# A Mamba, deformable-convolution, Fourier and attention stack on one core: the last image kept in SBUF between layers, its sampling positions made in two halves, and table stores of two chunks at a time

## The chip, the cores and the metric

The kernel runs on one core of a Trainium2 chip. The metric is the device time in microseconds of one execution, the median of several runs, lower is better. The core has five instruction queues that run side by side: PE (TensorE, matmuls), DVE (VectorE), ACT (ScalarE), POOL (GpSimd) and SP (SyncE, which only issues DMAs). Each of them runs its instructions in the order in which the program put them, and waits on semaphores for the others.

## What is computed

Four images of 96 channels and 64 by 64 pixels pass through four layers. Cut to what matters here:

```python
def reference(x, ...):                      # x: (4, 96, 64, 64)
    # layer 0: norm, projection, 3x3 depthwise conv, a selective scan in 4 directions
    #   h[t] = exp(delta[t] * A) * h[t-1] + delta[t] * u[t] * B[t];  y[t] = sum(h[t] * C[t])
    #   then norm, gate silu(z), projection;            x1 = x + layer0(x)
    # layer 1: group norm, then a deformable 3x3 convolution:
    n = group_norm(x1)
    off, mask = conv(n, offset_w), sigmoid(conv(n, mask_w))   # 9 taps for every pixel
    s = bilinear(n, base + off) * mask      # four neighbours of each of 9 positions
    x2 = x1 + einsum(weight, s) + bias
    # layer 2: t = x2;  t += fourier_mlp(norm(t));  t += quantized_ffn(norm(t))
    # layer 3: t += linear_attention(norm(t));      t += quantized_ffn(norm(t))
    return t
```

## The kernel before, in words

A channel-major image `[96, 4096]` is handled in eight chunks of 512 pixels (`CH`). Three streams of work are laid into the five queues by a planner that runs while the program is built. The first is the scan of layer 0 (`scan`): 1536 units, each one exponential on ACT (L1014), one product on DVE (L1034), one scan on DVE (L1042), one product on POOL (L1051) and matmuls (L1020, L1070). The second (`ends`) prepares the inputs of the scan for the next images, and then runs layers 2 and 3 of image 0, 1, 2, 3 in turn. The third (`middle`) runs, for each image in turn, what follows its scan (`behind`, which ends layer 0) and layer 1 (`Layer1.image`). A step of a stream carries an estimated cost, and `Clock.has_room` decides by it when a step is put in. `pipe` interleaves several chains of one stream; a chain takes and frees named slots (`takes`, `frees`). Nothing is put in a new order when the program runs.

For one image, the third stream does the following.

- `behind` works in four groups of two chunks, from the last chunks to the first. It loads the column-scan result of direction 3 with the axes exchanged (`yta`, `ytc`, L1112: for each channel and each of 64 columns one short run of rows), once for each half of the image. It adds that on POOL to the row result (L1134), norms, multiplies by the gate on POOL (L1180), projects, adds `x` (L1189) and stores `x1` to DRAM (L1191).
- `offsets` loads `x1` back (L1246), takes the group norm's statistics (eight `bn_stats`, L448), norms on ACT in place (L1260) and copies on POOL into a padded image (L1262). Then, for each chunk: nine matmuls of the offset convolution (L1278), and a transpose of the pixels, copied to `pix` (L1297) and stored eight times into a DRAM table (L1310), in which every pixel's entry holds its four neighbours (two tables, used in turn by the images). `pix` has two buffers.
- `positions` turns the offsets of the whole image into table indices `idx` and weights `wt`: one sigmoid on ACT (L1330) and sixteen operations on DVE (L1334 to L1363).
- `sample` gathers with an indirect DMA on POOL (L1383), 288 of them for an image, each of 128 pixels for one tap; weights them; transposes on PE (L1416); copies to `st` (L1424); multiplies by the convolution's weights (L1432); adds `x1`, loaded again by 256 pixels (L1429), on DVE (L1437); and stores `x2` (L1439). `g`, the gathered pixels, has six buffers of three taps; `st` has one.

Layers 2 and 3 begin with a load of the whole `x2` (L1825). Then comes a norm over the channels (`normed`: centring matmuls L485, sums of squares L501, Ln and Exp on ACT, three operations on DVE, spreading matmuls L527, a product L1613), and the Fourier part (L1551, L1510, L1576, L1590, L1595).

Only the last image has nothing to hide behind: when its scan is over, its layer 1 runs beside the layers 2 and 3 of image 2, and its own layers 2 and 3 run alone.

Of the kernel before, what the change touches and what calls it, by code (L numbers as in the profile page):

```python
# [8 lines left out]
F32 = mybir.dt.float32  # L9
# [262 lines left out]
def pipe(net, chains, width, every=0, lane=None, **tiles):  # L272
# [5 lines left out]
    while True:  # L278
# [9 lines left out]
        for n, chain in enumerate(active):  # L288
# [8 lines left out]
            if not all(free[tag] > 0 for tag in chain.takes):  # L297
                continue
# [5 lines left out]
        for tag in chain.takes:  # L304
            free[tag] -= 1
# [54 lines left out]
class Net:  # L360
# [3 lines left out]
    def __init__(self, ctx, tc, ins):  # L364
# [20 lines left out]
        self.sampling_last = False  # L385
        self.clock, self.known, self.streams, self.stream = Clock(), {}, [], None
# [56 lines left out]
    def group_norm_stats(self, x, pool, key, stats):  # L443

        nc = self.nc
        st = pool.tile([C, NCH, 6], F32, name=f"gnst{key}", tag="gnst")
        for j in range(NCH):
            nc.vector.bn_stats(st[:, j, :], x[:, j * CH : (j + 1) * CH])  # L448
            if j % 2:
                yield cost(dve=1.4)  # L450
# [22 lines left out]
    def centred(self, x, cen, dst, key, pool, bias=None, groups=(0, 1)):  # L473
# [7 lines left out]
        def chain(j):  # L481
            yield wait(new=True, takes="sq")
# [72 lines left out]
class Layer0:  # L555
# [438 lines left out]

    def fetch_step(self, u):
# [96 lines left out]
    def behind(self, b):  # L1092
# [6 lines left out]
        with (  # L1099
# [3 lines left out]
            cen_a, cen_c, wo_a, wo_c = (net.load(q, big) for q in ("cen_a", "cen_c", "wo_a", "wo_c"))  # L1103
            for j0 in range(NCH - HB, -1, -HB):
                if j0 % (NCH // 2) == NCH // 2 - HB:

                    h0 = H // 2 * (j0 * 2 // NCH)
                    yta = big.tile([128, W, H // 2], F32, name=f"yta{b}_{h0}", tag="yta")
                    ytc = big.tile([D2, W, H // 2], F32, name=f"ytc{b}_{h0}", tag="ytc")
                    for yt, c0 in ((yta, 0), (ytc, 128)):  # L1110
                        src = self.y_d[b][3][c0 : c0 + yt.shape[0]].rearrange("c (w h) -> c w h", h=H)
                        nc.sync.dma_start(yt, src[:, :, h0 : h0 + H // 2])  # L1112
                    yta_v, ytc_v = (t.rearrange("p w h -> p h w") for t in (yta, ytc))
                    yield wait(4.0)
                while not all((b, 2, j * CH // T) in self.summed for j in range(j0, j0 + HB)):
                    yield BLOCKED
                ca = big.tile([128, HB, CH], F32, name=f"ca{b}_{j0}", tag="ca")
# [5 lines left out]
                def centred(i):  # L1123
# [8 lines left out]
                    for y, yt in ((ya, yta_v), (yc, ytc_v)):  # L1132
                        y = y.rearrange("p (h w) -> p h w", w=W)
                        nc.gpsimd.tensor_add(y, y, yt[:, rs, :])  # L1134
                    yield cost(pool=3.1, new=True)
# [22 lines left out]
                nw = op.tile([128, CH], F32, name=f"nw{b}_{j0}", tag="nw", bufs=1)  # L1158
# [3 lines left out]
                def gated(i):  # L1162
# [16 lines left out]
                    for o, n, z, vg, vb in parts:  # L1179
                        nc.gpsimd.tensor_mul(o[:, i, :], o[:, i, :], z)  # L1180
# [760 lines left out]
```

## Time and profile before

| quantity | value |
|---|---|
| median of the 3 runs shown | 8472.4 us (8467.96 to 8479.75) |
| the profiled execution's own time | 8455.38 us |
| its span, first to last instruction | 8453.6 us |
| busy share of the span: PE, DVE, ACT, POOL | 76%, 81%, 58%, 66% |
| last unit of the scan starts on DVE | 7416.3 us |
| last `x1` of image 3 stored | 7481.0 us |
| first to last gather of image 3 starts | 7590.3 to 8023.3 us |
| image 2 written out | 7905.2 us |
| image 3's Fourier part begins | 8076.1 us |

The durations come from one profiled execution, which took 17 us less than the median of the runs. Times in the text are microseconds from the start of its span. The share of busy time mixes stages with different limits: up to 7416 the scan rules, after it the work of the last images.

### The profile page before, as it was taken

The page shows a single profiled execution, that of the slowest core. Times are in us where ns is not written, and L with a number is a line of the kernel's source. Part 1 is how long each engine was busy: PE and PEld are TensorE (multiplying, and loading weights), DVE is VectorE, ACT ScalarE, POOL GpSimd, SP SyncE. Part 2 cuts the span into 40 slices and gives each one's busy share as a digit, 9 for nine tenths or more (in the row PEclk, how much of TensorE's full clock was granted, in tenths as well). Part 3 has the DMA queues.
Part 4 walks back from the last instruction along what each step waited for, and adds up shares of the span by engine and source line. Part 5 has one row for each costly group of instructions (what it writes and reads, how often), then busy time and mean ns, then how long its engine had stood idle before and what let it go on. Part 6 is the DMA issues. An engine that isn't in the chain of part 4 may idle for free.

```text
span 8453.6 us, 96209 instructions
## 1 busy us (share of the span) xinstructions
PE 6424.4 (76%) x31848; PEld 2772.6 (33%) x31848; DVE 6826.4 (81%) x5122; ACT 4914.8 (58%) x8979; POOL 5621.2 (66%) x4308
## 2 busy tenths in 40 slices
PE   6765787678766777977767889777788777797587
PEld 2211221112222223321222555222455232464273
DVE  2799889987789898779888898898898988838714
ACT  5665566555567777855566677645576876333224
POOL 1566566665568888856578898766798997627700
PEclk8776787678767778977667898786798787898698
DMA  3676678877679888877788999776899897744410
GB/s 98 169 209 186 166 190 214 204 186 188 171 205 241 233 235 220 230 187 198 194 216 233 236 237 245 184 177 175 224 239 235 216 228 188 187 111 138 142 60 17
DMA packets 773926, 1608.27 MB, mean 190 GB/s; under 512 B 264082, under 2 KB 355758, under 8 KB 771223
## 3 DMA queue, kind: packets, MB, share of 16 engines
q10 hardware_dynamic: 244224, 843.17, 39.2%
q1 hardware_dynamic: 455478, 532.37, 24.4%
q0 software_dynamic: 73728, 226.57, 10.1%
q8 instruction: 256, 4.19, 0.2%
q14 instruction: 240, 1.96, 0.1%
HBM read 1345.43 MB, written 256.29 MB: 189 GB/s over the span
## 4 chain that ended last, share of the span: by engine, by line
PE 32%; DVE 26%; DMA 12%; POOL 11%; issue 9%; ACT 8%; SPq 2%; ACTq 1%; DVEq 0%; POOLq 0%
DVE da L1042 12%; POOL da L1051 7%; DVE db L1034 7%; PE pc L763 3%; DMA da<-de 3%; PE py L1070 3%; PE ps L1416 3%; PE f L1510 3%; POOL g L1383 3%; PE pd L1432 2%; PE db L1020 2%; ACT g L1395 2%; ACT da L1014 2%; DMA du<-du 1%; PE h L1551 1%
## 5 line engine op out<-in xcount | busy, mean ns | idle before, releaser
L1051 POOL TENSOR_TENSOR da<-da,bc 128x1024 f32<-128x1024 f32 x1536 | 3664.1, 2387 | 351.6 <-DVE da L1042 233.3
L1042 DVE TENSOR_TENSOR_SCAN da<-da,st,db 128x1024 f32<-128x1024 f32 x1152 | 2701.1, 2345 | 124.1 <-ACT da L1014 12.8
L1034 DVE TENSOR_TENSOR db<-db,bc 128x1024 f32<-128x1024 f32 x1536 | 1865.4, 1214 | 614.7 <-PE db L1020 613.1
L1014 ACT ACTIVATE da<-da,w_al 128x1024 f32<-128x1024 f32 x1536 | 1737.7, 1146 | 405.7 <-DMA da<-de 166.9
L1383 POOL DMA_INDIRECT g<-table,idx x1152 | 1206.8, 1048 | 360.2 <-issue 178.7
L1020 PE MATMUL db<-du,rep 24*128 24x512 bf16 x3072 | 683.7, 450 | 774.4 <-DVE da L1042 729.0
L1070 PE MATMUL py<-da,w_fold 128*32 128x512 f32 x6144 | 1091.8, 784 | 43.6 <-issue 25.2
L1395 ACT ACTIVATE g<-g,wt 128x96 f32<-128x96 f32 x3456 | 964.0, 365 | 107.1 <-DMA g<-table,idx 18.4
L1042 DVE TENSOR_TENSOR_SCAN da<-da,db 128x1024 f32<-128x1024 f32 x384 | 877.0, 2284 | 54.7 <-ACT da L1014 19.6
L1416 PE MATMUL ps<-w_ident,g 128*96 128x128 f32 x3744 | 680.7, 325 | 252.3 <-issue 107.6
L1020 PEld LDWEIGHTS <-rep 24*128 24x128 bf16 x3072 | 147.3, 93 | 1839.2 <-DVE da L1042 1164.6
L851 POOL TENSOR_TENSOR lw<-lw,w 128x512 f32<-128x512 f32 x192 | 244.0, 1271 | 700.5 <-DVE w L849 667.8
L1416 PEld LDWEIGHTS ps<-w_ident,g 128*96 128x96 f32 x3744 | 483.5, 144 | 601.3 <-issue 178.9
L1049 POOL COPY st<-da 128x1 f32<-128x1 f32 x1152 | 232.2, 202 | 674.1 <-DVE da L1042 655.8
L763 PE MATMUL pc<-pad,wc 96*128 96x512 f32 x1152 | 576.3, 636 | 7.0 <-DVE rl L853 5.3
L1424 ACT COPY st<-ps 96x384 f32<-96x384 f32 x384 | 180.2, 472 | 572.3 <-PE ps L1416 533.8
L882 PE MATMUL pr<-ex,w_ident 128*128 128x512 f32 x384 | 311.2, 904 | 125.5 <-DVE ex L866 53.5
L1432 PE MATMUL pd<-st,wdc 96*128 96x256 f32 x1152 | 323.7, 434 | 12.7 <-DVE rl L853 6.0
L763 PEld LDWEIGHTS pc<-pad,wc 96*128 96x128 f32 x1152 | 217.9, 200 | 318.6 <-issue 303.5
L840 PE MATMUL pd<-xd,w_dtw 103*64 103x512 f32 (+1 forms) x512 | 273.4, 799 | 47.0 <-DVE rl L853 15.6
L1070 PEld LDWEIGHTS py<-da,w_fold 128*32 128x32 f32 x6144 | 158.1, 124 | 381.1 <-issue 300.3
L1432 PEld LDWEIGHTS pd<-st,wdc 96*128 96x128 f32 x1152 | 243.2, 219 | 104.2 <-issue 39.5
(259 smaller groups left out, 8631.4 us busy)
## 6 DMA issues: line engine op xcount, KB each, us to landing
da<-de ACTq DMA_DIRECT2D x1536, 512.0 KB
du<-du SPq DMA_DIRECT2D x1536, 96.0 KB
bc<-bcd SPq DMA_DIRECT2D x128, 512.0 KB
y<-yb SPq DMA_DIRECT2D x384, 128.0 KB
de<-rl SPq DMA_DIRECT2D x128, 256.0 KB
m<-in_dft SPq DMA_DIRECT2D x128, 256.0 KB
ad<-y ACTq DMA_DIRECT2D x192, 128.0 KB
table<-pix SPq DMA_DIRECT2D x256, 96.0 KB
```

Of the source, the lines that this page charges most:

```text
L763: nc.tensor.matmul(pp, lhsT=wc[:, q, g * 128 : (g + 1) * 128], rhs=pad[:, r0 + dy : r0 + dy + NR, dx : dx + W], start=(q == 0), stop=(q == 8),
L882: nc.tensor.matmul(pr, lhsT=net.ident, rhs=ex, start=True, stop=False)
L1014: self.net.nc.scalar.activation(u.da, u.da, AF.Exp, scale=self.al[:, a : a + 1])
L1020: self.net.nc.tensor.matmul(db[:, h, :], lhsT=self.rep[64 * u.q + 32 * h : 64 * u.q + 32 * h + 24], rhs=u.du[64 * u.q + 32 * h : 64 * u.q ...
L1034: self.net.nc.vector.tensor_mul(u.db, u.db, u.bc[:, 0, :])
L1042: nc.vector.tensor_tensor_scan(u.along(u.hh), u.along(u.da), u.along(u.db), first, ALU.mult, ALU.add)
L1051: self.net.nc.gpsimd.tensor_mul(u.hh, u.hh, u.bc[:, 1, :])
L1070: nc.tensor.matmul(py[p0 : p0 + 32], lhsT=self.fold[:, u.i, :], rhs=hc[:, h * CH : (h + 1) * CH], start=u.sums["add"] is None and u.i == 0 ...
L1383: nc.gpsimd.indirect_dma_start(out=g[:, k, :], out_offset=None, in_=self.tables[b % 2], in_offset=bass.IndirectOffsetOnAxis(ap=idx[:, n : ...
L1395: nc.scalar.activation(pixel, pixel, AF.Identity, scale=wt[:, n, c : c + 1])
L1416: nc.tensor.matmul(pt[:, k, :], lhsT=g[:, k, c * C : (c + 1) * C], rhs=net.ident, is_transpose=True, start=(c == 0), stop=(c == corners - 1),)
L1432: nc.tensor.matmul(po, lhsT=wdc[:, k, :], rhs=st[:, k, :], start=(k == 0), stop=(k == 8))
```

## The change

For image 3 alone:

- `x1` is loaded with `x` once at the start of `behind`, gets its additions in place and stays in SBUF; its `bn_stats` are taken chunk by chunk. The store and the two reloads of `x1` go. `x2` is made in place in the same tile, which layers 2 and 3 use as `t`; the store and the reload of `x2` go.
- `yta` and `ytc` are loaded once for each of the four groups (16 rows) rather than for each half (32 rows).
- In the last group the additions and the gates are on DVE rather than POOL.
- `positions` runs twice for half of the image each: the first as soon as four chunks of offsets are done, the second at the head of `sample`.
- Tiles of `sample` and `offsets` take slots of the scan's rings (`da`, `bc`), which are then free; `pix` has four, `st` and `xo` two.
- Layer 2's first norm runs by halves, its centring of each chunk allowed as soon as that chunk of `x2` is there (`arriving`).

For every image:

- ACT writes the normed chunk straight into the padded image; the POOL copy goes.
- The table is written ahead of the offset convolutions. Its pixels are transposed by matmuls of one image row (64 columns), two chunks to one `pix`; each of the eight stores covers two chunks. For images 0 to 2 `pix` has one buffer of the double size.

```diff
--- before.py
+++ after.py
 def behind(self, b, x1=None, st=None):
+            if x1 is not None:
+                nc.sync.dma_start(x1, ins["x"][b])
             for j0 in range(NCH - HB, -1, -HB):
-                if j0 % (NCH // 2) == NCH // 2 - HB:
+                rows = H // 2 if x1 is None else H // 4
+                if (j0 + HB) * NR % rows == 0:
...
-                        nc.sync.dma_start(yt, src[:, :, h0 : h0 + H // 2])
+                        nc.sync.dma_start(yt, src[:, :, h0 : h0 + rows])
...
+                ends = b == B - 1 and j0 == 0
-                        nc.gpsimd.tensor_add(y, y, yt[:, rs, :])
+                        (nc.vector if ends else nc.gpsimd).tensor_add(y, y, yt[:, rs, :])
...
-                        nc.gpsimd.tensor_mul(o[:, i, :], o[:, i, :], z)
+                        (nc.vector if ends else nc.gpsimd).tensor_mul(o[:, i, :], o[:, i, :], z)
...
                     nc.vector.tensor_add(xr, po[:C], xr)
+                        nc.vector.bn_stats(st[:, j, :], xr)
 def offsets(...):
             def filled(j):
-                nc.scalar.activation(x[:, cs], x[:, cs], AF.Identity, scale=rstd, bias=nmr)
-                nc.gpsimd.tensor_copy(
-                    pad[:, 1 + j * NR : 1 + (j + 1) * NR, 1 : 1 + W],
-                    x[:, cs].rearrange("p (h w) -> p h w", w=W),
-                )
+                nc.scalar.activation(Layer0.rows(pad, j), plain_rows(x, j), AF.Identity, scale=rstd, bias=nmr)
+            def table(jj):
+                yield wait(new=True, takes="pix")
+                if place_of is None:
+                    pix = pre.tile([128, 8, C], F32, name=f"pix{b}_{jj}", tag="pix")
+                else:
+                    pix = l0.ring(f"pix{b}_{jj}", 8 * C).rearrange("p (q c) -> p q c", c=C)
+                for h in range(2):
+                    pt = net.mm(f"pt{b}_{jj}_{h}")[:, : 4 * C].rearrange("p (q c) -> p q c", c=C)
+                    for q in range(4):
+                        for r in range(2):
+                            row = pad[:, 1 + 16 * jj + 8 * h + 2 * q + r, 1 : 1 + W]
+                            nc.tensor.matmul(pt[64 * r : 64 * r + 64, q, :], lhsT=row,
+                                             rhs=net.ident[:C, :C], start=True, stop=True)
+                    nc.scalar.copy(pix[:, 4 * h : 4 * h + 4, :], pt)
+                for q in range(4):
+                    dy, dx = divmod(q, 2)
+                    for r in range(2):
+                        y0 = 2 + 16 * jj + r - dy
+                        dst = v[y0 : y0 + 15 : 2, 2 - dx : 2 - dx + W, q * C : (q + 1) * C]
+                        nc.sync.dma_start(dst.rearrange("t w d -> w t d"), pix[64 * r : 64 * r + 64])
...
-            yield from pipe(self.net, (chunk(j) for j in range(NCH)), 3, oc=1, pix=2)
+            def chains():
+                for jj in range(NCH // 2):
+                    yield table(jj)
+                for j in range(NCH):
+                    yield chunk(j)
+                    if place_of is not None and j == 3:
+                        yield place_of(0)
+            yield from pipe(net, chains(), 4, every=-99, oc=min(deep, 2), pix=deep, po=min(deep, 2), om0=-3, om1=-3)
 def sample(self, b, x, idx, wt, l0, place_of):
-                yield wait(takes="g")
+                yield wait(takes="g half" if last and t >= 16 else "g")
...
-                xr = gp.tile([C, 256], F32, name=f"xr1_{b}_{j}", tag="xr")
-                nc.sync.dma_start(xr, self.x1[b][:, cs])
+                if last:
+                    xr = xo = x[:, cs]
...
-                nc.sync.dma_start(self.x2[b][:, cs], xo)
+                if not last:
+                    nc.sync.dma_start(self.x2[b][:, cs], xo)
+                elif j % 2:
+                    net.arrived[f"x{j // 2}"] = 1
...
+            def chains():
+                if last:
+                    yield place_of(1)
+                for t in range(4 * NCH):
+                    for k0 in (0, 3, 6):
+                        yield taps(t, k0)
-            yield from pipe(self.net, chains, 8, g=6, st=1, xo=1)
+            yield from pipe(self.net, chains(), 8, lane=taps.__code__, g=6, st=1 + last, xo=1 + last)
 Fourier.run:
-                yield from normed(net, t, tl, f"2_{b}", pool)
+                if b == B - 1:
+                    for r in range(2):
+                        yield from normed(net, t, tl, f"2_{b}_{r}", pool, (r,), True)
 Layers23.image:
-        while b not in self.net.sampled:
+        while b not in net.sampled if b < B - 1 else net.last_image is None:
             yield BLOCKED
...
+            else:
+                t = net.last_image
             yield from self.fourier.run(b, t)
```

## The prediction

> **What bounds the kernel now.** I read the page first. Its 40 slices of 211 us show where the kinds of work change; the group of the gathers gives the price of one.
>
> ```profile
> DVE  2799889987789898779888898898898988838714
> POOL 1566566665568888856578898766798997627700
> L1383 POOL DMA_INDIRECT g<-table,idx x1152 | 1206.8, 1048 | 360.2 <-issue 178.7
> ```
>
> DVE stays at 8 or 9 tenths through slice 35: the scan rules up to 7416 us. What the change touches for the last image comes after that, so I cut that stretch into stages:
>
> ```profile
> core 0: us, PE busy (x) PEld busy (x) DVE busy (x) ACT busy (x) POOL busy (x), PEclk, DMA share, GB/s
> 7437.00:7481.00 44.00, 42.55 (x328) 27.27 (x326) 21.26 (x30) 10.98 (x18) 11.29 (x8) 1.00 0.20 56
> 7481.00:7509.00 28.00, 24.43 (x380) 24.00 (x377) 6.41 (x16) 7.11 (x15) 0.59 (x4) 0.88 0.40 106
> 7509.00:7528.00 19.00, 16.85 (x132) 12.39 (x132) 0.00 (x0) 11.36 (x22) 4.88 (x8) 1.00 0.46 140
> 7528.00:7577.00 49.00, 48.14 (x512) 34.86 (x512) 0.00 (x0) 14.52 (x34) 0.00 (x0) 1.00 0.70 141
> 7577.00:7590.00 13.00, 11.56 (x142) 11.29 (x140) 8.78 (x16) 7.33 (x11) 0.00 (x0) 0.85 0.33 105
> 7590.00:7905.00 315.00, 225.54 (x854) 125.51 (x853) 253.89 (x368) 99.90 (x203) 252.61 (x206) 0.78 0.47 139
> 7905.00:8036.00 131.00, 56.45 (x202) 41.28 (x201) 81.60 (x100) 15.08 (x32) 97.95 (x85) 0.64 0.50 148
> 8036.00:8076.00 40.00, 24.15 (x48) 8.58 (x48) 7.64 (x12) 10.19 (x19) 0.00 (x0) 0.74 0.17 42
> ```
>
> The rows are: last group of `behind`; `x1` out and in again with its statistics; padding; table stores; positions; sampling beside image 2; sampling alone; `x2` out and in with the norm. In the five rows before sampling POOL is nearly idle for 153 us, with the gathers ahead of it; PE is full, but with image 2's Fourier part, which is not yet due. In the sampling rows POOL is busy 0.80 and 0.75; its gathers, counted alone, are 205 in the first (one per 1.54 us) and 84 in 119 us of the second (1.42). PE is at 0.72 and 0.43 there. So what counts is when the first gather starts, how fast gathers follow, and what stands after the last. The timeline of the SP queue and the chain of waits give the parts:
>
> ```profile
> 7528.41 5.54 SPq L1310 DMA_DIRECT2D table<-pix  x8
> 7540.72 34.47 SPq L1310 DMA_DIRECT2D table<-pix  x48
> ```
>
> ```profile
> 8036.32 1.66 DMA x<-xo
> 8038.11 8.73 DMA t<-x
> 8046.88 7.02 PE lnc L485 x8
> 8065.56 9.65 PE lnb L527 x16
> ```
>
> A table store costs SP 0.69 to 0.72 us, 64 of them 49 us with the last landing. The last `x2` takes 10.4 us through DRAM, and the norm another 29.
>
> **The Trainium skill.** *Perfetto Trace Analysis*, "Tensor Engine Instruction (MATMUL, LD_WEIGHTS)", says that ACT, DVE and GpSimd are strict FIFO: a copy that waits on ACT holds up the exponentials behind it. The trace is consistent: no group shows an overtaking. *DMA: Bandwidth & Descriptors*, "Anatomy of one DMA", gives about 2 us fixed for a DMA, mostly completion; here the last table store was complete 2.4 us after its issue ended at 7574.6. The same page, "Why small descriptors are slow (HBM only)", charges each packet an overhead; in the trace's packets 128 bytes took 22 ns and 384 bytes 29.
>
> **The change, part by part.** *Start of sampling.* (a) In the last group eight POOL operations (1.56 us each at L1134, 1.3 to 1.4 at L1180) become DVE ones of about 0.69 (as L1173): the last `x1` at 7477 instead of 7481, -4. (b) `x1`'s store (2.1), load (8.9), and seven of eight `bn_stats` (4.84 in all) go; the aggregate, at 7497.4 before, comes at 7478. (c) From there to the norm's factors took 11.5 us, the two small matmuls waiting behind image 2 on PE; I keep 11: 7489. (d) Eight norms on ACT of 0.81, with image 2's copies between: 10 us, 7499; the POOL copy after the last (0.6) goes. (e) Transposes for a first `pix` and two copies of 0.48: stores begin at 7502. (f) Now 32 stores of 512 runs of 384 bytes. No row shows such a store: below, it costs the 0.72 us of the smaller one; above, twice that; the packets need 512 x 29 ns / 16 engines = 0.93. I take 1.0: 32 us, and 2.4 to land, 7536. (g) Eight offset convolutions (36 matmuls of four took 5.35 us) run on PE meanwhile. The positions of a half need one sigmoid with two table loads (3 us) and operations half as wide (10 us for sixteen before, some 6 now); begun at about 7520 they have indices by 7529, under the stores. First gather 7537 instead of 7590.3: **-53** (bounds -63 with (f) at its lower end, -39 at its upper). The second half's positions, 6 us on DVE ahead of the first weighting, lie under the first three gathers and six `g` buffers.
>
> *Sampling.* 288 gathers, as before. Image 2 has more left: in the changed program's order it ends with tile 26 of 32 instead of tile 22, so four tiles of nine gathers run at 1.54 rather than 1.42 us: +4. Half of the last norm beside the last tiles: +2 (0 to 6). A memset of `tl` (L1530, 3.51 us on POOL), which stood after the last gather, now stands among them, five tiles from the end: +3.5. And since `tl` now takes image 2's place in SBUF, the memset waits in the changed program for image 2's output store. 1.5 MB took 8.7 to 8.9 us as a load; the memset comes six gathers (9 us) after the tile that image 2's end falls to: +2.5 (0 to 20 if image 2 runs late), with all later gathers behind it. **+12**. The second `st` and `xo` buffer: 0, since the wait table has POOL waiting for nothing of them.
>
> *After sampling.* From the last `xo` (8035.8) to the first Fourier matmul (8076.1) are 40.3 us. What stays is one chunk: `xo` 0.5, centring 1.8, square 0.6, sums 2.2, Ln, Exp, Square 2.0, three DVE operations 2.0, four spreads 4.8, product 0.7, hops: 16. The other half was done beside the gathers. **-24** (-20 to -26).
>
> *The scan's side.* (h) The run of ACT copies to `pix` in images 0 to 2. Before, six of these waited 21 us for stores and two masks 17. Now each of three copies an image waits for all eight stores of the previous `pix`, which has one buffer. Sixteen stores of the same bytes took SP 15 us in the scan at 2296, eight 6.0; so 12 to 15 and 2.4 to land, less the 5 to 13 us that the program order puts between: some 7 us, nine times. Queued behind are exponentials, which DVE's scan waits for. Start and end times of all units in the trace give the cover: an exponential ends a median 6 us before its scan starts. Lost then: about 2 us each, less what the old waits cost: +12 (-5 to +60). Where the cover is gone the wait counts in full. (i) `yta` and `ytc` by quarters: four loads instead of two, each again 12,288 runs, of 64 bytes now. What one costs:
>
> ```profile
> 7300.38 14.16 SPq L1112 DMA_DIRECT2D ytc<-y  x1
> DVE db L1034 <- PE db L1020: 19.2, 2, 17.2
> ```
>
> SP stood 14 us, and a Fourier matmul waiting for its matrix behind that on SP held PE, so DVE idled 17. By the changed order one new load falls in the middle of the scan's last direction, with only `du` loads and `y` stores behind it (0 to 17, I take 6), the other into the last 15 us of units, ahead of Fourier matrices (0 to 10, I take 4); the early 1.5 MB load of `x` replaces smaller ones: +2. **+24** with (h). (j) 24 POOL copies of 0.61 us, and as many SP issues saved in images 0 to 2 as table stores halve: 0 (to -10), as DVE bounds the scan. DRAM traffic saved in sampling: 0, since DMA is at 0.5 there.
>
> Sum: -53 + 12 - 24 + 24 = **-41**. From the profiled execution's 8455 (span 8453.6 and 2 us around it) to 8414. The median shown is 17 higher, which I leave on both sides: 8472 - 41 = **8431**.
>
> **The rivals.** *More* (0.08): the stores at 0.72 us and the scan untouched: -63 + 12 - 24 - 5 = -80, 8392. For it: ACT has 6 us of cover. *Stores set the pace* (0.14): 1.44 us each, -39, sum -27, 8445; the packets alone forbid much less than 0.93. *The start is given back in sampling* (0.11): with PE 0.95 full through the first eight tiles (image 2's 48 us of Fourier matmuls on top of 0.5 of sampling's own), or the memset held 20 us or more, the last gather moves by only some 15 us rather than 41: -15 - 24 + 24 = -15, 8457. Against it: over the whole stretch PE is busy 417 of 600 us, so the work fits. *Slower* (0.07): the waits of ACT for `pix` in images 0 to 2 pass whole to the scan. At 10 to 13 us nine times, 90 to 117, with +12 of (i) and -65 of the rest: +37 to +64, about 8520. It decides above 7.8 us lost per wait ((65 - 12 + 17) / 9). For it: the scan has only two units of exponentials ahead; against it: cover of 6 us, and DVE idle at 13% anyway. That the change doesn't do what it says can be set aside: in its order the first gather waits for the first half's `idx` and the table stores alone.
>
> **How the numbers follow.** The forecast has 0.60, at 8400 to 8455. A measurement of this kernel can tell 0.2%, 17 us, from no change: faster means below 8455.5. All of the first two rivals and nearly all of the forecast lie there; of the third a part: 0.79. Same 0.13, slower 0.08. The range reaches from 8386 (below it a part of *More*) to 8472, which leaves out the slower rival and little else.
>
> **What would show it.** Right: the first gather of image 3 some 53 us closer to the scan's end (153 us after 7437 before); table stores of 0.9 to 1.1 us; 288 gathers in 440 to 450 us; 16 us from the last `xo` to the first `h`. The scan's last unit at 7416 to 7450. Wrong: a last unit beyond 7480 (ACT waiting for `pix`), gathers slower than 1.6 us, a memset waiting over 20 us, or a last `x1` not earlier against the last unit.

## The result and the profile after

The changed kernel took 8519.15 us (median of 9 runs, 8495.66 to 8545.25) against 8484.34 us (9 runs, 8467.96 to 8507.12): ratio 1.0047, 95% interval 1.0026 to 1.0067. It is slower by some 40 us, where 41 us less was forecast. The profiled execution took 8543.74 us (span 8542.0), near the upper end of its runs; a second profile of the same kernel (`e1_again` below) had a span of 8496.4. A single profile stands up to 40 us off the median of its kernel's runs (25 above here, 26 above in e2, 35 below in e3, 40 above in e17), so stages are compared here over several profiles, and kernels by their ratios.

The page of the changed kernel, the lines that answer to those of before (the 40 slices are of 213.6 us here):

```profile
DVE  2799889987799888788799888787888888856724
POOL 1566567656478898756588888665788897526800
L1493 POOL DMA_INDIRECT g<-table,idx x1152 | 1204.1, 1045 | 398.3 <-issue 179.0
```

A gather costs what it did, but DVE falls to 8 and 7 tenths in the slices after the middle, where it had 8 and 9. The stages of the last image, cut as before (busy times of PE, PEld, DVE, ACT and POOL; granted clock; DMA share):

```profile
7555.00:7590.00 35.00, 34.33 (x217) 19.30 (x216) 18.55 (x29) 10.85 (x18) 0.43 (x4) 1.00 0.11 32
7590.00:7607.00 17.00, 16.59 (x237) 16.30 (x234) 6.64 (x18) 2.36 (x7) 0.22 (x2) 1.00 0.03 8
7607.00:7621.00 14.00, 14.00 (x247) 14.00 (x246) 0.00 (x0) 10.00 (x17) 0.00 (x0) 1.00 0.01 2
7621.00:7661.00 40.00, 39.51 (x370) 20.98 (x367) 5.24 (x16) 13.71 (x27) 0.32 (x1) 0.96 0.70 185
7661.00:8069.00 408.00, 286.63 (x1471) 183.97 (x1469) 289.91 (x423) 124.26 (x251) 288.16 (x242) 0.78 0.44 130
8069.00:8152.00 83.00, 48.62 (x160) 30.85 (x161) 54.07 (x68) 18.37 (x37) 56.99 (x48) 0.71 0.44 133
8152.00:8165.00 13.00, 8.10 (x21) 2.57 (x21) 4.61 (x7) 3.01 (x5) 0.00 (x0) 0.87 0.00 0
```

The rows are: last group of `behind`; statistics and factors; padding and transposes; stores, offset convolutions and positions; sampling beside image 2; sampling alone; what stands after the last `x2`. The row of `x1` through DRAM is gone, and the last row is 13 us rather than 40. The SP queue with the table stores, and the chain of waits after the last sampled chunk:

```profile
7621.85 25.58 SPq L1370 DMA_DIRECT2D table<-pix  x32
7647.48 2.34 SPq L1699 DMA_DIRECT2D m<-in_dft  x4
```

```profile
8151.09 0.49 DVE x L1551
8151.63 1.12 PE lnc L489 x2
8158.56 5.39 PE lnb L531 x8
8164.77 18.89 PE h L1678 x256
```

32 stores took 25.6 us, 0.80 each, and from the last addition to the first Fourier matmul there are 13.7 us: no load of `x`, one chunk's norm. So the stages named in the prediction came out about as long as named, but the first gather waited for something else than it said. These are the last operations ahead of it, the first half's `idx`, the last offset convolutions, and the gather:

```profile
7650.87 0.23 DVE L1456 TENSOR_SCALAR idx<-fr 128x144 uint32<-128x144 f32 x1
7652.80 7.04 PE L1381 MATMUL po<-pad,w_wom 96*32 96x512 f32 x36
7660.69 1.02 POOL L1493 DMA_INDIRECT g<-table,idx  x1 [70.47 <-PE po L1381]
```

The indices were ready at 7651.1 and the last store was issued by 7647.4; the gather started at 7660.7, 0.8 us after the last of the eight convolutions. In the kernel the tile `g` is opened when the pool that holds the padded image is closed, so that `g` probably takes the space that the convolutions still read; no run tests this.

The table counts the stages from the start of the scan's last unit.

| us after the scan's last unit | before | forecast | changed | e1 |
|---|---|---|---|---|
| last `x1` | 63.9 | 61 | 54.5 | 54.5 |
| aggregate | 81.1 | 62 | 58.8 | 58.7 |
| first norm into the padded image | 93.0 | 73 | 72.1 | 72.0 |
| first table store | 112.1 | 86 | 87.0 | 86.8 |
| first gather | 174.0 | 121 | 125.8 | 124.0 |
| first to last gather | 433 | 445 | 478 | 443 |
| last `x2` to first Fourier matmul | 40.3 | 16 | 13.7 | 13.7 |
| end | 1037 | 972 | 1007 | 971 |
| **the last unit itself, at** | 7416 | 7440 | **7535** | **7526** |

Nearly all of the miss is in the last row. (Some of its 110 to 119 us is scatter: before's profile is a fast execution, 8455 us, where its nine runs beside the changed kernel have a median of 8484.) The loss has a place: units 0 to 1056 of the 1536 took 5065 us in all of before, the changed kernel and e1; units 1056 to 1152 took 443 us before, 485 and 489 in the two profiles of the changed kernel; 1152 to 1248 took 442, then 472 and 473. The busy times over units 1056 to 1152, first before, then changed:

```profile
5249.00:5691.00 442.00, 332.31 (x1326) 109.97 (x1326) 397.64 (x278) 244.75 (x420) 313.67 (x231) 0.80 0.78 187
```

```profile
5245.00:5730.00 485.00, 373.11 (x1886) 156.99 (x1886) 392.96 (x261) 262.53 (x470) 325.79 (x242) 0.80 0.78 186
```

DVE is busy about as long (398 and 393 us), so the 43 us more are time in which DVE stands idle. PE has 560 matmul records more in it (1886 for 1326). 384 of them are the `f` matmuls of image 0's Fourier part, which before stood ahead of unit 1056. Nobody edited anything there. What moved is the planner's order. Layers 2 and 3 of images 0, 1 and 2 began at units 903, 1174 and 1473 in the program before, and begin at 939, 1203 and 1480 in the changed one.

### The profile page after: what moved, and what is told of

It reads as the page before. It is cut to its first block, busy times and chain, and to the rows that moved or that the text cites. A ratio compares the mean times of both kernels' runs of the same rounds, so it can differ in the third digit from the quotient of the medians.

```text
span 8542.0 us, 96681 instructions
## 1 busy us (share of the span) xinstructions
PE 6494.3 (76%) x32232; PEld 2815.5 (33%) x32232; DVE 6852.1 (80%) x5149; ACT 4920.9 (58%) x8985; POOL 5587.5 (65%) x4268
## 4 chain that ended last, share of the span: by engine, by line
PE 31%; DVE 29%; DMA 12%; POOL 9%; issue 8%; ACT 8%; SPq 2%; ACTq 1%; another core or an unknown queue 0%; DVEq 0%; POOLq 0%
DVE da L1053 13%; DVE db L1045 7%; POOL da L1062 6%; PE pc L767 4%; PE f L1633 3%; PE py L1081 3%; PE ps L1526 3%; DMA da<-de 3%; ACT g L1505 2%; PE db L1031 2%; PE pd L1545 2%; ACT da L1025 2%; POOL g L1493 2%; DMA m<-in_dft 2%; DMA du<-du 1%
## 5 line engine op out<-in xcount | busy, mean ns | idle before, releaser
L1053 DVE TENSOR_TENSOR_SCAN da<-da,db 128x1024 f32<-128x1024 f32 x384 | 877.2, 2284 | 56.0 <-ACT da L1025 20.7
L1526 PE MATMUL ps<-w_ident,g 128*96 128x128 f32 x3744 | 701.4, 332 | 220.7 <-issue 69.7
L1526 PEld LDWEIGHTS ps<-w_ident,g 128*96 128x96 f32 x3744 | 501.6, 148 | 552.6 <-ACT g L1505 160.8
```

Of the source, the lines that this page charges most:

```text
L1053: nc.vector.tensor_tensor_scan(u.along(u.hh), u.along(u.da), u.along(u.db), first, ALU.mult, ALU.add)
L1526: nc.tensor.matmul(pt[:, k, :], lhsT=g[:, k, c * C : (c + 1) * C], rhs=net.ident, is_transpose=True, start=(c == 0), stop=(c == corners - 1),)
```

## The experiments

All ratios are to runs of the kernel before on the same chip. e1 to e4 and e13 to e18 ran on one chip, e5 to e8 on a second, e9 to e12 on a third. A difference in us between two runs below is the difference of their ratios, times 8460 us, where nothing else is said. **Theory A**: the edits to the table changed the costs that the planner books, it lays the two side streams differently into the scan, and that order is slower. **Theory B**, the *Slower* rival of the prediction: ACT waits for the single `pix`. **Theory C**: image 3's own parts.

**e1**, the changed kernel again.

> The changed kernel once more, for a second profile and a second set of times. Every theory: 1.003 to 1.007 of the time before. What is asked is how much of the lateness of the scan's last unit (7535 us in the first profile of the changed kernel, against 7416 before) comes back: all three theories explain a loss there, so I expect 7480 to 7540, and the first gather 48 us closer to it than before.

1.0034 (1.0022 to 1.0045), 8488.4 us, the last unit at 7526: as expected. Its stages are in the table above.

**e2**, image 3's parts alone:

```diff
-                    yield from self.offsets(b, None, None, om, None, l0)
+                    yield from self.offsets_by_chunk(b, om)   # `offsets` of the kernel before
```

> Images 0 to 2 make their table as before the change (chunk by chunk, POOL copies, two buffers of pix); image 3 has every part of the change. The program order up to image 3 is then that of the kernel before, the layers 2 and 3 of image 0 at unit 903 of the scan again (939 in the changed kernel). Theory A, the planner's order: the edits to the table make the planner put the preparation of images 2 and 3, and with it layers 2 and 3 of images 0 to 2, later in the program; with the old table this is gone: 0.993 to 0.996 of before, last unit at 7415 to 7445. Theory B, ACT waiting for the single pix: gone too, the same numbers, so this run doesn't part A from B. Theory C, the loss comes from image 3's own parts (x loaded early, yta by quarters): it stays, 1.002 to 1.006, last unit beyond 7480.

0.9963 (0.9954 to 0.9973), 34 us faster than before by the medians; last unit at 7447, in a profile that is the slowest of its 19 runs. Both lie just outside the range of Theories A and B (0.996 and 7445) and far from that of C: Theory C falls. The gain is only half of the 65 that image 3's steps were to give. In its profile the first gather came 155.6 us after the last unit, not 121, though the last store was issued at +116. SP first, then PE, behind the padding:

```profile
7538.46 25.30 SPq L1370 DMA_DIRECT2D table<-pix  x32
7563.86 6.01 SPq L1774 DMA_DIRECT2D m<-in_dft  x5
```

```profile
7549.76 4.46 PE L1381 MATMUL po<-pad,w_wom 96*32 96x512 f32 x28
7567.50 2.02 PE L1778 MATMUL zp<-d,m 128*128 128x96 f32 x8 [13.27 <-DMA m<-in_dft]
```

The stores are one block on SP; image 2's matrix `m` is issued only behind it; image 2's matmul waits 13.3 us for `m`, and image 3's remaining offset convolutions stand behind that matmul on PE. The first half's `idx` came at +141 instead of +116, the last convolution ended at +155, and the gather followed it. In e1's order no such matmul stood between the convolutions, and the first gather came at +124.

**e3**, one booked cost more in the changed kernel, no instruction:

```diff
                 nc.scalar.activation(Layer0.rows(pad, j), plain_rows(x, j), AF.Identity, scale=rstd, bias=nmr)
                 yield cost(act=0.8)
+                if place_of is None:
+                    yield cost(pool=0.7)
```

> The changed kernel with one line more: for images 0 to 2 the planner books 0.7 us of POOL, for which no instruction is issued, after each normed chunk, as it did when a copy stood there. Table, single pix and all waits of ACT stay. In the order that comes out, layers 2 and 3 of image 0 begin at unit 898 rather than 939. Theory A (order): the loss goes, 0.992 to 0.997 of before, last unit at 7410 to 7450. Theory B (ACT's waits for pix): it stays, 1.002 to 1.007, last unit beyond 7480. Theory C (image 3's own parts): it stays as well.

0.9993 (0.9979 to 1.0007), between the ranges of A and of B and C: 35 us better than e1 with the same instructions. The last unit came at 7442, as A had it, but in the fastest of the 14 runs, 35 us below their median. Theory A is shown for the 35 us; 25 us to e2 stay.

**e4**, the order alone, in the kernel before (`units` counts the scan's units):

```diff
-        while b not in self.net.sampled:
+        while b not in self.net.sampled or net.clock.units < (938, 0, 0, 0)[b]:
             yield BLOCKED
```

> The kernel before with one condition more: layers 2 and 3 of image 0 may not begin before unit 938 of the scan (903 before), as late as in the changed kernel; every instruction and every table is that of the kernel before. Theory A (order): the scan's last unit comes 60 to 120 us later, at 7475 to 7535, and the whole takes 1.008 to 1.014 of before, since no gain of image 3 stands against it. Theories B and C: 0.998 to 1.002, last unit at 7410 to 7430.

1.009 (1.0069 to 1.011): 77 us lost by the medians, with every instruction kept. Units 1056 to 1152 took 472 us. The range for the last unit (7475 to 7535) misses: in the profile, the fastest of six runs, it came at 7446, 30 us later than before, and another 21 us were lost behind it (first gather at +189 for +174). So an order costs in image 3's part too, not in the scan alone.

**e5 to e8** ask for the rest between e3 and e2, and for the stores. e5, in e3:

```diff
-                x = pre.tile([C, L], F32, name=f"x1_{b}", tag="x")
+                room = pre.tile([128, L], F32, name=f"x1_{b}", tag="x")
+                x = room[:C]
...
-                    pix = pre.tile([128, 8, C], F32, name=f"pix{b}_{jj}", tag="pix")
+                    pix = room[:, 768 * jj : 768 * (jj + 1)].rearrange("p (q c) -> p q c", c=C)
```

> As e3 (changed kernel, booked POOL cost, order with layers 2 and 3 of image 0 at unit 898), but for images 0 to 2 the four pix lie side by side in the space of x, which is free once the padded image is filled: ACT waits for no table store. Program order is that of e3, instruction by instruction. e3 stood at 0.9993 of before, e2 at 0.9963; this asks for those 25 us. Theory W (nine waits of ACT for pix, 7 to 10 us each, pass to the scan): 0.994 to 0.997. Theory O (e3's own order) and theory P (PE's row transposes): no change, 0.998 to 1.001.

0.9969 (0.9956 to 0.9982): W holds, 20 us against e3 (on another chip, the intervals overlapping a little). The waits for the stores that it took away, in e1 and then in e3 (us in total, times, longest; waits that ended with another releaser are in other rows):

```profile
ACT pix L1363 <- DMA table<-pix: 45.3, 6, 9.6
```

```profile
ACT pix L1365 <- DMA table<-pix: 30.2, 3, 11.1
```

Whatever ended them, ACT stood 70 us ahead of the nine first copies in e1 and 79 in e3. So about a quarter of the waiting (20 of 79 us) passed to the whole in e3's order.

**e6**, PE's price of the new transposes, in e2 with the order pinned:

```diff
-                nc.gpsimd.tensor_copy(pad[...], x[:, cs]...)          # ACT writes pad itself
                 yield cost(pool=0.7)
...
-                    nc.tensor.transpose(pt[:, q, :], x[:, 128 * t : 128 * t + 128], net.ident[:C, :C])
+                    for r in range(2):
+                        row = pad[:, 1 + NR * j + 2 * q + r, 1 : 1 + W]
+                        nc.tensor.matmul(pt[64 * r : 64 * r + 64, q, :], lhsT=row, rhs=net.ident[:C, :C], ...)
```

> As e2 (images 0 to 2 with the old table, order of the kernel before), but in images 0 to 2 ACT writes the normed chunk into the padded image (the POOL copies go) and the pixels come to pix by two matmuls of one image row each in place of one transpose of 128 pixels, as in the changed kernel. pix keeps two buffers, the order is pinned by booking POOL's cost as before. PE's work on pt in one image was 32 x 0.246 = 7.9 us and becomes 128 records x 0.287 = 37 us. Theory P (this price is paid by the scan): 3 x 29 us, half of it or more: 1.000 to 1.006 of before. Theories W and O: it is hidden, 0.995 to 0.998 as e2.

0.9969 (0.9958 to 0.998), e2 within the intervals. So the two edits together, PE's transposes and the POOL copies that go, cost nothing that can be seen; that each costs nothing is not shown, since a gain from the copies could cover a loss from the transposes. The rows of `pt`, before and in e1 (ns: least, median, most):

```profile
L1295 PE MATMUL pt<-w_ident,x x128: 243/246/423, 2269.4 to 7561.0; 96*128 96x96 f32 x128
```

```profile
L1356 PE MATMUL pt<-w_ident,pad x512: 244/287/424, 2252.2 to 7616.9; 96*64 96x96 f32 x171
```

The price was also smaller than expected. The 37 us for an image add up the times of records that overlap. The time in which PE had any such record running is 19.1 us for all four images before and 36.9 in e1: some 4 us more for an image, not 29.

**e7** and **e8**, sixteen of image 3's stores on POOL, in e2 and in e5 (there `if r and place_of is not None`, which keeps the other images' stores on SP):

```diff
-                        nc.sync.dma_start(dst.rearrange("t w d -> w t d"), pix[64 * r : 64 * r + 64])
+                        (nc.gpsimd if r else nc.sync).dma_start(dst.rearrange("t w d -> w t d"), pix[64 * r : 64 * r + 64])
```

> As e2, but of image 3's 32 table stores sixteen (the odd rows) are issued by POOL, which is idle then. In e2's profile SP issued them as one block of 25 us; image 2's loads of m stood behind it, and an image 2 matmul waiting for m (13.3 us) held PE with the offset convolutions of image 3 behind it, so that the first gather came 39 us after the last store. If that is the chain: stores over some 12 us earlier, PE's wait gone, first gather 125 to 140 us after the scan's last unit rather than 155.6, and 0.992 to 0.995 of before. Rival: POOL pays more than 1.5 us for a store, or the gain is given back in sampling beside image 2: 0.9955 to 0.998.

> e5 and e7's edit together, the whole change kept: e5's number less what e7 gains over e2. If W and the SP chain both hold: 0.989 to 0.994. If neither: 0.998 to 1.001.

0.9958 (0.9945 to 0.9971) and 0.9963 (0.9952 to 0.9974): no gain over e2 and e5 that the intervals show. e7 misses its first range and lies in the rival's, though for neither of the rival's reasons; e8 lies in neither of its two. e7's profile shows why. Its stores by queue (ns: least, median, most; first and last start):

```profile
L1370 SPq DMA_DIRECT2D table<-pix x16: 628/1371/5078, 7521.2 to 7546.8; - x16
L1370 POOL DMA_DIRECT2D table<-pix x16: 687/689/772, 7521.5 to 7533.9; - x16
```

SP took 26 us for sixteen, as long as for 32: a store held it 1.37 us. The DMA engines were 0.87 to 0.91 busy in these 26 us, and 0.87 in e2's block of 32. So the issuing was not the limit, the transfers were. `m` still came behind them, and the first gather still at +157.8.

**e9 to e12** try Theory A in the form that e3 and e4 suggest: the later layers 2 and 3 begin, the slower. e9 (changed kernel), e10 (before) and e11 (e5) ask the preparing stream first until image 0's layers 2 and 3 begin (`net.preparing` is true until then):

```diff
-            return any([stream.step() for stream in (streams if net.sampling_last else streams[::-1])])
+            return any([stream.step() for stream in (streams if net.sampling_last or net.preparing else streams[::-1])])
```

e12 is e4 with 920 in place of 938.

> The changed kernel, all of its instructions and waits kept; only the planner's order of the two streams is turned: until layers 2 and 3 of image 0 begin, the stream that prepares images 1 to 3 is asked first and the sampling second (reversed in both kernels). Layers 2 and 3 of image 0 then begin at unit 837 of the scan (939 in the changed kernel, 903 before), sampling of image 0 ends at unit 721 rather than 700. Theory A (how late layers 2 and 3 begin sets the scan's end): 41 units earlier gave 35 us (e3), 36 units later cost 77 (e4); 100 units give 60 to 110 us from 1.0034: 0.990 to 0.997 of before. Rival D (a fixed sum of work: what leaves the late units makes the early ones longer): 1.000 to 1.005.

> The same turn of the order in the kernel before: layers 2 and 3 of image 0 at unit 826 instead of 903, nothing else. Theory A: 0.985 to 0.995 of before, the scan's last unit 40 to 110 us earlier. Rival D: 0.998 to 1.003.

> The same turn with e5 (no waits of ACT for the stores in images 0 to 2): layers 2 and 3 of image 0 at unit 843, 898 in e5. Theory A: e5's 0.9969 less 40 to 90 us: 0.986 to 0.992, below both kernels. Rival D: 0.995 to 0.999.

> As e4 but layers 2 and 3 of image 0 held until unit 920, half as long (18 units after the 903 of before). Theory A with a loss in proportion to the delay: 1.003 to 1.006 of before. If instead the loss depends on what the late work then meets (image 2's loads and matmuls from unit 1083 on), it need not be in proportion: anything from 0.999 to 1.009.

1.0094 (1.0071 to 1.0116), 1.0139 (1.0116 to 1.0162), 1.0029 (1.0018 to 1.004) and 1.0082 (1.0061 to 1.0103). e9, e10 and e11 miss both of their ranges: earlier is slower too. e12 misses the loss in proportion and lies within the wide range given for a loss that depends on what the late work meets: half the delay costs as much as the whole. That the order costs is confirmed; that lateness sets its price falls.

**e13 to e15** ask whether the price is the Fourier work that comes to stand in units 1056 to 1152. e13 (before), e14 (e4) and e15 (changed) leave one transform out, with its costs still booked:

```diff
-                for part in range(2):
+                for part in range(0 if key == "2_0_1" else 2):
...
-            nc.scalar.copy(d[:, :, c0 : c0 + 8], pt.rearrange("p c j -> p j c"))
+            if key != "2_0_1":
+                nc.scalar.copy(d[:, :, c0 : c0 + 8], pt.rearrange("p c j -> p j c"))
```

> A yardstick: the kernel before without the last inverse transform of image 0's Fourier part (192 matmuls of f and 12 copies of ACT left out; the planner books them as before, so the order is the same). In this order they stand ahead of unit 1056 of the scan, in a stretch where the scan lost little. Theory F (a new order costs time where Fourier matmuls come to stand in units 1056 to 1152): leaving them out here gains little, 0.997 to 1.000 of before. Theory G (PE work costs the same wherever it stands): 0.991 to 0.995.

> e4 (before, layers 2 and 3 of image 0 held until unit 938; it took 1.009 of before) without the same transform, which stands in units 1056 to 1152 there. Theory F: 30 to 50 us gained, 1.003 to 1.006, and the 472 us of units 1056 to 1152 fall to 440 to 455. Theory G: as much as e13 gains, no more. Rival H (the cost of the held order is spread over many places): 1.007 to 1.009, at most 10 us gained in units 1056 to 1152.

> The changed kernel (1.0034 of before) without the same transform, in units 1056 to 1152 here too. Theory F: 30 to 50 us gained, 0.997 to 1.000; units 1056 to 1152 in 440 to 460 us rather than 485. Rival H: 1.001 to 1.003.

0.9997 (0.9984 to 1.0009), 1.0062 (1.0046 to 1.0078), 1.0023 (1.0013 to 1.0034). In the order of before the transform is free, so Theory G falls. In e4's order it is worth 24 us (units 1056 to 1152 in 458 rather than 472 us), in the changed order 9 (478 rather than 485 and 489); both intervals overlap those of the kernels with the transform, so neither gain is certain. e14 lies between the ranges of F and H, e15 in that of H. So Theory F is right for a part at most; most of the price is elsewhere, as H said.

**e16**, in e2, an honest time for the strided loads:

```diff
-                    yield wait(4.0)      # behind yta, ytc
+                    yield wait(20.0)
```

> e2 (0.9963) with the planner told that yta and ytc take 20 us to land rather than 4: the traces show POOL waiting 17 to 21 us for them and PE, in order behind it, 11 to 17 us (images 0 and 1). The order shifts by 1 to 13 units (layers 2 and 3 of image 0 at unit 908, 903 in e2). If those stops of PE pass to the scan: 0.991 to 0.995. If they are hidden and only the order changes: within 0.004 of e2 either way.

1.0015 (1.0004 to 1.0026). POOL's wait for image 0's load fell from 17.3 to 8.7 us and image 1's from 20.7 to 14.2, the scan was 45 us ahead of e2 at unit 768, and 26 behind at its last unit, in an order whose stages had moved by 1 to 13 units. The loss is outside both ranges given: by these two profiles, what the waits gave back, the rest of the order took.

**e17** and **e18** ask what sets the costly order off, and whether order and waits add up. e17, in the kernel before, with POOL's copies kept (it unbooks the eight of image 3 too; e3 books only those of images 0 to 2):

```diff
                     x[:, cs].rearrange("p (h w) -> p h w", w=W),
                 )
-                yield cost(pool=0.7)
```

e18 is the changed kernel with e5's edit and nothing booked.

> The kernel before, every instruction kept, the POOL copies too; only the planner no longer books 0.7 us of POOL for each of them. Its order moves as in the changed kernel: layers 2 and 3 of image 0 at unit 938 (903 before, 939 changed). It is e3 the other way round. If the lost booking is what costs (35 us between the changed kernel and e3): 1.003 to 1.007 of before, loss after unit 1056 of the scan. If what costs needs the new table's instructions as well: 0.999 to 1.002.

> The changed kernel (1.0034) in its own order, with the four pix of images 0 to 2 in the space of x as in e5, so that ACT waits for no table store; nothing booked. If order and waits add up, as the sum over e1, e3, e5 assumes: 1.000 to 1.002. If the waits are hidden in this order: 1.003 to 1.004.

e17: 1.0079 (1.0064 to 1.0094), somewhat more than its range. The instructions of the kernel before, less one number in the planner, are some 67 us slower (63 by the medians). Units 1056 to 1152 of its profile, the slowest of seven runs:

```profile
5236.00:5726.00 490.00, 377.75 (x1914) 165.46 (x1910) 389.63 (x261) 262.51 (x472) 323.35 (x239) 0.78 0.79 183
```

That is the changed kernel's row almost number for number: 490 us, 378 of PE, 390 of DVE. Its waits in that stretch, against before's (first fence: before):

```profile
DVE db L1034 <- PE db L1020: 25.5, 13, 7.6
POOL ya L1134 <- DMA ya<-y: 3.3, 2, 1.7
```

```profile
DVE db L1034 <- PE db L1020: 53.7, 24, 6.7
POOL ya L1134 <- DMA ya<-y: 31.0, 3, 18.4
```

DVE waits twice as long for the product's matmul, with PE busy 378 us instead of 332, and POOL waits 31 us for image 2's loads.

e18: 0.9988 (0.9976 to 0.9999), 39 us below e1, outside both of its ranges: in this order the waits cost twice what they cost in e3's. This figure leans on the ratios. The medians of e1 and e18 are 8488 and 8486 us; it is the kernel before that took 38 us longer beside e18 (8497 for 8460), on the same chip.

The orders side by side (units of the scan at which layers 2 and 3 of images 0, 1, 2 begin):

| instructions of | order | units | ratio |
|---|---|---|---|
| before | its own | 903, 1174, 1473 | 1 |
| before | e17, copy not booked | 938, 1191, 1479 | 1.0079 |
| before | e12, held | 921, 1183, 1477 | 1.0082 |
| before | e4, held | 939, 1206, 1487 | 1.009 |
| before | e10, preparation first | 826, 1124, 1466 | 1.0139 |
| image 3 only | as before | 903, 1174, 1473 | 0.9963 |
| image 3 only | e16, longer wait | 908, 1178, 1474 | 1.0015 |
| changed | its own | 939, 1203, 1480 | 1.0034 |
| changed | e3, copy booked | 898, 1173, 1469 | 0.9993 |
| changed | e9, preparation first | 837, 1138, 1470 | 1.0094 |
| changed, no waits for `pix` | its own (e18) | 939, 1203, 1480 | 0.9988 |
| changed, no waits for `pix` | e5, copy booked | 898, 1173, 1469 | 0.9969 |
| changed, no waits for `pix` | e11, preparation first | 843 (image 0) | 1.0029 |

Four of the changed kernel's rows part the two prices:

| | ACT waits for `pix` | no waits |
|---|---|---|
| its own order | 1.0034 (e1) | 0.9988 (e18) |
| the order with the copy booked | 0.9993 (e3) | 0.9969 (e5) |

The versions that beat both kernels clearly are e2, e5, e6, e7 and e8, at 0.9958 to 0.9969, which the intervals don't part; all keep an order like that of before.

## Why the prediction was wrong

**The sum against what was measured.** Forecast: image 3's steps -53 + 12 - 24, the scan's side +24, together -41. Measured by the ratios: e1 +29; e2, image 3 alone in the order of before, -31; e5, the whole change with the copy booked and no waits for `pix`, -26. From e5 to e1 are 55 us, for the order and the waits together, where the sum had +12. Without these 12 the sum stood at -53, so e5 lacks 27 more: its profile shows 14 of them in the first gather (+135 for +121); the rest has no run of its own.

**The step that failed is (j), and with it (h), in what both took for granted: that the program's order stays, or that a new one costs the scan nothing.** (j) priced the removal of 24 POOL copies at 0, "as DVE bounds the scan". For the instructions nothing speaks against it: e6 takes them out, with the transposes put in, and sees no difference. But each copy also had a booked cost, and without it the planner drew another order. No term of the sum stood for that. The working had the changed order at hand and used it for image 2's end, the memset and the loads of (i), but priced everything else in the place it had before. Taken alone, the lost booking costs 67 us (e17). In the changed kernel it costs 35 us with ACT's waits (e1 less e3), and without them 16 (e18 less e5, 0.9988 and 0.9969, intervals overlapping).

**(h) was right in mechanism, and too small in price for the order that came.** It had nine waits of some 7 us and 2 us lost by each, +12 after what the old waits cost. The nine waits were there, 70 us in e1 (7.8 each). They cost 20 us in e3's order (2.2 each, as forecast) and by the ratios 39 in the changed one (4.3 each): order and waits do not simply add. The bound of +60 held them.

**(i) and the early load of `x`** cannot be seen apart. SP stood 9.42 us at the quarter load at 7408 and 5.51 at 7526, and DVE's longest wait for PE near the first was 8.5 us; e2's last unit is 31 us later in one profile, within the scatter of profiles.

```profile
7407.99 9.42 SPq L1126 DMA_DIRECT2D ytc<-y  x1
7526.06 5.51 SPq L1126 DMA_DIRECT2D ytc<-y  x1
```

**Start of sampling**: (a) was worth more (9 us for 4), and (b) to (e) came within 4 us. In (f) a store took 0.80 us, between the lower end 0.72 and the 1.0 taken. The packet price under it was too high, and with it the saying that packets forbid much less than 0.93: a packet of 384 bytes took some 24 ns in the changed kernel's block of stores, not 29. (The 2.4 us to land count from the start of the last store's issue at 7574.6, not from its end, and the section of *DMA: Bandwidth & Descriptors* that the prediction names from the Trainium skill describes DMAs issued by GpSimd, while these are SP's.) In (g) the two conditions of the first gather, `idx` and the stores, were not all: it also waited for the last offset convolution, 8 to 10 us beyond the first half's `idx` in the changed kernel and 15 in e2. So the positions by halves gained less than they could. That the first gather came 48 to 50 us closer to the scan's end, for 53, is luck in part: stores that were over 6 us earlier than forecast paid for most of that wait. In e2 (18 us closer) and e3 (36) it came out: that the offset convolutions "run on PE meanwhile" needed that no image 2 matmul waiting for `m` stands among them. That is why e2 keeps only half of image 3's gain.

**Sampling**: +10 in e1 (443 for 433) against +12, but 478 in the first profile. There the first ten tiles took 159 us, against 136 before and 133 in e1. It is not the third rival's full PE: PE was busy 51 of the first 79 us there and 59 of the first 66 in e1. PE idled more, not less, and ACT stood 42 us for something that the trace doesn't name, in e1 not at all. The same stretch took 169 and 159 us in the profiles of e17 and e18, and 130 to 143 in all others, with orders and instructions of every kind; what causes it stays open. The memset waited for nothing (idle 0.0 us ahead of it). PE's "417 of 600 us", held against that rival, are 426 by the working's own rows. **After sampling**: -26.6 against -24.

**The rival *Slower*** gave 8520 and the median is 8519. That is luck: its point, 7.8 us lost per wait, was not reached; 2.2 to 4.3 were, and the order paid the rest. With the waits and e3's order the kernel is at 0.9993, with its own order and no waits at 0.9988, either about even with before; it took both to make it slower.

**What stays open** is what in an order costs. Every order drawn anew for unchanged or nearly unchanged instructions was slower than the one it replaced (e4, e10, e12, e16, e17; e9 against e1, e11 against e5), but for e3's, whose stages lie within 5 units of those of before. Fourier work in units 1056 to 1152 accounts for 9 to 24 us at most (e14, e15), and e9 lost 37 us in the same units with no Fourier matmul in them. Another feature of that stretch was not tested but goes with the loss in the profiles: the longest stop of POOL in it, ahead of the addition of a strided load (L1134), which also stops PE (in e9 25 us and 20). In the eight profiles where that stop was 18 to 25 us (the changed kernel's two, e4, e9, e10, e15, e17, e18) these units took 472 to 493 us; in the eight where it was under 4 (before, e2, e3, e5 to e8, e13) 438 to 450; in four with 8 to 16 us (e11, e12, e14, e16) 445 to 459. It suits e9, and e15, where the transform went and the stop stayed. A run that takes away this stop alone would have to show it, and it would not price the whole: e9 and e10 had lost 53 and 65 us ahead of unit 1056, and e4 lost 21 us after the scan. No feature was found that prices an order ahead of a run.

## What to carry to other kernels

Where a program's order is computed from booked costs, an edit has two prices: that of its instructions, and that of the order it makes the planner draw; set the two orders side by side over the whole program, and keep the order fixed (a booked cost without an instruction does it) while the edit is timed. If the order of the kernel before was good, a redrawn one is likelier to lose: here 0.4 to 1.4%, as much as the 0.3 to 0.4% that the edit earned in a good order, or more. A buffer that is saved turns up as waits on the engine that fills it; here the space of an input that was already used up gave four buffers for nothing.

## What the runs showed of the hardware that was not expected

- Table stores of 512 runs of 384 bytes: 32 took 25.3 to 25.6 us from one queue (0.79 to 0.80 us each), and 26 us when two queues issued sixteen each, SP then being held 1.37 us by a store and POOL 0.69, with the DMA engines 0.87 to 0.91 busy either way. 32 x 512 runs in 25.5 us are 25 ns of one of 16 engines for each run.
- A transpose of 128 pixels from a plain image was one matmul record of 0.246 us. As two f32 matmuls of 64 columns against the identity it was four records of 0.287 us (512 for 128 in all). The records overlap: the time in which PE had one of them running grew from 19.1 to 36.9 us, 1.9 times and not the 4.7 that the sum of the records would give.
- An execution of one and the same program varied by 0.7% (e1: 8462 to 8519 us in 22 runs), and the two profiles of the changed kernel differ by 46 us, 34 of them in the sampling beside image 2, where the trace doesn't name what ACT waited for in 42 us.
